# Two mixture-of-experts stages put into a written order, with image pairs on halves of the TensorE array

## The chip, the cores and the metric

The kernel runs on one core of a Trainium2 chip. The metric is the device time of one execution in microseconds (us). The kernel before has a median of 12985.0 us over three runs (12982.07 to 13003.0). One further execution was taken by the profiler; all views of the profile come from it, and its own time is 12885.25 us.

## What is computed

The reference is a network of four layers on an image batch of shape 4 x 128 x 48 x 48: a state-space convolution block (layer 0), a deformable convolution (layer 1), then a linear-attention block with a mixture of experts (layer 2) and a causal attention with a second mixture of experts (layer 3). The change is in the two mixtures alone. Both compute, on tokens t (4 images, L = 2304 tokens, 128 channels), t + experts(norm(t)):

```python
logits = einsum('bsd,ed->bse', x, gate_w) + gate_b        # 64 experts
probs = softmax(logits, axis=1)                           # over the tokens
vals, idx = top_k(probs.transpose(0, 2, 1), 8)            # 8 tokens per expert
pooled = einsum('bked,bke->bed', gathered, topv)
h = gelu(einsum('ebd,edh->ebh', [pooled, 1], weight1))    # hidden size 512
out = einsum('ebh,eho->ebo', [h, 1], weight2)
outputs[b, idx] += out * topv
```

Each expert so weighs its eight tokens of an image into one vector, sends it through its own two matrices, and adds the result back to these tokens. The last mixture writes the network's output, with channels ahead of tokens.

## The kernel before

All arithmetic is in f32. The residual T stays in SBUF as 72 tiles of 128 tokens x 128 channels (18 tiles per image). `program` runs layer 0, layer 1, layer 2, `experts` for "f2_", layer 3 and `experts` for "f3_". The layers 2 and 3 stand in a section `manual_schedule(engines=ORDERED)`, in which TensorE (PE), ACT, DVE and POOL issue in the order of the program; SP, which issues most DMAs, isn't in that set. `_experts` (L1567) stands outside such a section in the kernel before: a scheduler merges its instructions by priority. Its steps are:

- **Gates**, image by image, in blocks of 384 tokens (three tiles; six blocks per image). `moments` (L973) takes bn_stats and bn_aggr of each of 18 tiles on DVE (L980, L981) and the power -0.5 on POOL (L984). ACT normalises each tile to xh (L1605), PE turns three tiles (L1612), DVE copies them to xT (L1614), PE multiplies by the 64 gate columns (L1616) into one half of PSUM's partitions, and ACT adds the bias and writes the logits G (L1617). Images 2q and 2q+1 share G[:, q, :], 64 partitions each.
- **Selection**, per pair q: maximum (L1626), exponential with its sum on ACT (L1629), scaling by 1/sum (L1631), the eight largest (L1634), match_replace and a subtraction that leaves the eight largest and zeros (L1636, L1637), 18 transposes of G with copies to GT on ACT (L1642, L1643), and 18 products per image that pool the tokens (L1648). A product in f32 is two passes on PE, so the profile counts it twice; a transpose is one.
- **Groups**: 64 experts in 16 groups of four. Per group 1 MB each of w1 and w2 is loaded (L1660, L1663, four buffers each). The four experts stand on four strips of 32 columns: w1 product (L1668), bias product with b1 (L1677), Gelu on ACT (L1679), four transposes (L1682), copy hT on DVE (L1684), w2 product (L1688), bias product with b2 (L1697), copy o4 on ACT (L1699), one transpose (L1701) and a copy into oT on DVE (L1702).
- **Output**, per pair, image and block. Each product takes one image's 64 rows of G and o. In "f2_" three products of 64 rows (L1718) are added to T on DVE (L1725). In "f3_" three tiles of T are turned (L1729) and one product (L1737) is accumulated on them in PSUM; the sum is copied on DVE or ACT and goes out by a DMA (L1745).

Of the kernel before, what the change touches and what calls it, by code (L numbers as in the profile page):

```python
# [15 lines left out]
F32 = mybir.dt.float32  # L16
I32 = mybir.dt.int32
AF = mybir.ActivationFunctionType
ALU = mybir.AluOpType
# [4 lines left out]
P = 128  # L24
NB = 4
# [944 lines left out]
            nc.scalar.activation(T[:, b * NT + i, :], out, AF.Relu)  # L970


def moments(env, pool, src):  # L973

    nc = env.nc
    n = src.shape[1]
    st = pool.tile([P, n, nc.vector.BN_STATS_DIM], F32, name="bn_st", tag="bn_st")
    mv = pool.tile([P, n, nc.vector.BN_AGGR_DIM], F32, name="bn_mv", tag="bn_mv")
    for i in range(n):
        nc.vector.bn_stats(out=st[:, i, :], in_=src[:, i, :])  # L980
        nc.vector.bn_aggr(out=mv[:, i, :], in_=st[:, i, :])  # L981
    rstd = pool.tile([P, n], F32, name="rstd", tag="rstd")
    nc.vector.tensor_scalar_add(rstd, mv[:, :, 1], 1e-5)
    nc.gpsimd.tensor_tensor(rstd, rstd, env.half[:, :n], ALU.pow)  # L984
    return mv[:, :, 0], rstd


def normed_T(env, sp, ps, src, mean, rstd, i0, out, scale=1.0, bias=None):

    nc = env.nc  # L990
# [576 lines left out]
def _experts(ctx, env, io, pre, T, final):  # L1567
# [10 lines left out]
    def psum(*shape):  # L1578
        return ps.tile(list(shape), F32, name="psum", tag="ps")
# [12 lines left out]

    xh = cp.tile([P, NB * NT, C], F32, name="xh")
    G = cp.tile([P, npair, L], F32, name="G")
    for b in range(NB):
        Tb = T[:, b * NT : (b + 1) * NT, :]
        mean, rstd = moments(env, sp, Tb)
        shift = sp.tile([P, NT], F32, name="shift")
        nc.vector.scalar_tensor_tensor(shift, mean, -1.0, rstd, op0=ALU.mult, op1=ALU.mult)
        half = slice(b % 2 * NE, (b % 2 + 1) * NE)  # L1600
        for j in range(NBLK):
            pt = psum(P, BLK)
            for g in range(G3):
                i = j * G3 + g
                nc.scalar.activation(  # L1605
                    xh[:, b * NT + i, :],
                    Tb[:, i, :],
                    AF.Identity,
                    bias=shift[:, i : i + 1],
                    scale=rstd[:, i : i + 1],  # L1610
                )
                nc.tensor.transpose(pt[:, bass.ts(g, P)], xh[:, b * NT + i, :], ident)  # L1612
            xT = sp.tile([P, BLK], F32, name="xT")
            nc.vector.tensor_copy(xT, pt)  # L1614
            pg = psum(P, BLK)
            nc.tensor.matmul(pg[half, :], gate_w, xT, start=True, stop=True)  # L1616
            nc.scalar.activation(  # L1617
                G[half, b // 2, bass.ts(j, BLK)], pg[half, :], AF.Identity, bias=gate_b[half, :]
            )

    pooled = cp.tile([P, NE, QC], F32, name="pooled")
    nc.gpsimd.memset(pooled, 0.0)
    for q in range(npair):
        p = G[:, q, :]
        mx = sp.tile([P, 1], F32, name="mx")
        nc.vector.reduce_max(mx, p, axis=AX.X)  # L1626
        nc.vector.tensor_scalar_mul(mx, mx, -1.0)
        total = sp.tile([P, 1], F32, name="total")
        nc.scalar.activation(p, p, AF.Exp, bias=mx, accum_out=total)  # L1629
        nc.vector.reciprocal(total, total)  # L1630
        nc.vector.tensor_scalar_mul(p, p, total)  # L1631

        top = sp.tile([P, TOPK], F32, name="top")
        nc.vector.max(out=top, in_=p)  # L1634
        rest = sp.tile([P, L], F32, name="rest", bufs=1)
        nc.vector.match_replace(out=rest, in_to_replace=top, in_values=p, imm_value=0.0)  # L1636
        nc.vector.tensor_sub(p, p, rest)  # L1637
        GT = sp.tile([P, NT, P], F32, name="GT", bufs=1)
        for j in range(NBLK):
            pt = psum(P, G3, P)  # L1640
            for g in range(G3):
                nc.tensor.transpose(pt[:, g, :], p[:, bass.ts(j * G3 + g, P)], ident)  # L1642
            nc.scalar.copy(GT[:, j * G3 : (j + 1) * G3, :], pt)  # L1643
        for r in range(2):
            b = 2 * q + r
            pp = psum(P, NE)
            for i in range(NT):
                nc.tensor.matmul(  # L1648
                    pp,
                    xh[:, b * NT + i, :],  # L1650
                    GT[:, i, r * NE : (r + 1) * NE],
                    start=i == 0,
                    stop=i == NT - 1,
                )
            nc.vector.tensor_copy(pooled[:, :, b], pp)

    oT = cp.tile([P, NB, NE], F32, name="oT")
    for e0 in range(0, NE, EG):
        w1 = wp.tile([P, EG, HID], F32, name="w1")
        nc.sync.dma_start(w1, w1_io[e0 : e0 + EG, :C, :].rearrange("e d f -> d e f"))  # L1660

        w2 = wp.tile([P, EG, NHC, C], F32, name="w2")
        nc.sync.dma_start(  # L1663
            w2, w2_io[e0 : e0 + EG, :HID, :].rearrange("e (f c) o -> f e c o", c=NHC)
        )
        ph = psum(P, HID)
        for g in range(EG):
            nc.tensor.matmul(  # L1668
                ph[g * QC : (g + 1) * QC, :],
                pooled[:, e0 + g, :],  # L1670
                w1[:, g, :],
                start=True,
                stop=False,
            )
        for g in range(EG):
            own = ident[:NE, e0 + g : e0 + g + 1].to_broadcast([NE, QC])
            nc.tensor.matmul(ph[g * QC : (g + 1) * QC, :], own, b1, start=False, stop=True)  # L1677
        h = sp.tile([P, P, NHC], F32, name="h")
        nc.scalar.activation(h.rearrange("p f c -> p (f c)"), ph, AF.Gelu)  # L1679
        pt = psum(P, NHC, P)  # L1680
        for c in range(NHC):
            nc.tensor.transpose(pt[:, c, :], h[:, :, c], ident)  # L1682
        hT = sp.tile([P, NHC, P], F32, name="hT")
        nc.vector.tensor_copy(hT, pt)  # L1684
        po = psum(P, C)
        for c in range(NHC):
            for g in range(EG):
                nc.tensor.matmul(  # L1688
                    po[g * QC : (g + 1) * QC, :],
                    hT[:, c, g * QC : (g + 1) * QC],  # L1690
                    w2[:, g, c, :],
                    start=c == 0,
                    stop=False,
                )
        for g in range(EG):
            own = ident[:NE, e0 + g : e0 + g + 1].to_broadcast([NE, QC])
            nc.tensor.matmul(po[g * QC : (g + 1) * QC, :], own, b2, start=False, stop=True)  # L1697
        o4 = sp.tile([P, C], F32, name="o4")
        nc.scalar.copy(o4, po)  # L1699
        pt = psum(P, EG, QC)  # L1700
        nc.tensor.transpose(pt.rearrange("p g t -> p (g t)"), o4, ident)  # L1701
        nc.vector.tensor_copy(  # L1702
            oT[:, :, e0 : e0 + EG].rearrange("p b e -> p e b"), pt[:, :, :NB]
        )
    for q in range(npair):
        pt = psum(P, C)
        nc.tensor.transpose(pt, oT[:, 2 * q : 2 * q + 2, :].rearrange("p b e -> p (b e)"), ident)
        o = sp.tile([P, C], F32, name="o")
        nc.scalar.copy(o, pt)
        for r in range(2):  # L1710
            half = slice(r * NE, (r + 1) * NE)
            b = 2 * q + r
            for j in range(NBLK):
                i0 = b * NT + j * G3
                if final is None:
                    pp = psum(P, G3, C)
                    for g in range(G3):
                        nc.tensor.matmul(  # L1718
                            pp[:, g, :],
                            G[half, q, bass.ts(j * G3 + g, P)],  # L1720
                            o[half, :],
                            start=True,
                            stop=True,
                        )
                    nc.vector.tensor_add(T[:, i0 : i0 + G3, :], T[:, i0 : i0 + G3, :], pp)  # L1725
                    continue
                pp = psum(P, BLK)
                for g in range(G3):
                    nc.tensor.matmul(  # L1729
                        pp[:, bass.ts(g, P)],  # L1730
                        T[:, i0 + g, :],
                        ident,
                        is_transpose=True,
                        start=g == 0,
                        stop=False,
                    )
                nc.tensor.matmul(  # L1737
                    pp, o[half, :], G[half, q, bass.ts(j, BLK)], start=False, stop=True
                )
                res = sp.tile([P, BLK], F32, name="res", bufs=4)  # L1740
                if j % 2:
                    nc.scalar.copy(res, pp)
                else:
                    nc.vector.tensor_copy(res, pp)
                nc.sync.dma_start(final[b][:, bass.ts(j, BLK)], res)  # L1745


def layer3(env, io, T):
# [480 lines left out]
```

## Time and profile before

| what | us |
|---|---|
| median of three runs | 12985.0 |
| the profiled execution, its own time | 12885.25 |
| its span, first to last instruction | 12883.3 |
| PE busy, share of the span | 11151.3, 87% |
| DVE busy | 8493.7, 66% |
| ACT busy | 6929.4, 54% |
| POOL busy | 4401.5, 34% |
| first experts stage, first bn_stats to last addition to T | 10733.2 to 11024.6 |
| layer 3 | to about 12563 |
| last experts stage, first bn_stats to the end | 12563.6 to 12883.3 |

The page divides the span into 40 slices of 322 us; the two stages are slices 34 and 40. Busy time on PE is modelled from the size of an instruction, so a busy PE isn't a PE at its peak. "PEclk" or "clock" is the share of TensorE's full clock that was granted in a stretch; it is 0.935 over the span. In a row of a group, "128*64 128x384" is a stationary operand of 128 rows and 64 columns, with an output of 128 partitions x 384 elements. The "chain" is the work that ended last, followed back from the last instruction: start us, length us, engine, tile and line.

### The profile page before, as it was taken

How to read it: one execution, taken by the hardware profiler on the slowest of the kernel's cores; microseconds unless marked ns; L12 is line 12 of the kernel's file. 1: busy time of each engine (PE TensorE's matmuls, PEld its weight loads, DVE VectorE, ACT ScalarE, POOL GpSimd, SP SyncE). 2: the span in 40 equal slices, each digit the busy share in tenths (PEclk: the TensorE clock that was granted, in tenths of full speed). 3: DMA queues.
4: the chain of work that ended last, by engine and by line, in shares of the span. 5: the costliest groups of instructions: out<-in, count | busy, mean ns of one | idle time of the engine just before them, and what ended most of it. 6: DMA issues, size and time to landing. Idle time of an engine off the chain costs nothing. (4 is left out here: it accounts for less than half of the span.)

```text
span 12883.3 us, 192724 instructions
## 1 busy us (share of the span) xinstructions
PE 11151.3 (87%) x71150; PEld 8431.5 (65%) x71150; DVE 8493.7 (66%) x15424; ACT 6929.4 (54%) x13281; POOL 4401.5 (34%) x4727
## 2 busy tenths in 40 slices
PE   6879788878797887689799999999999997899997
PEld 4667666766676666488677787777877774333333
DVE  4998889888988899455555666566665653444442
ACT  3777777777777777311155655555565653123322
POOL 1443333333333344277643333333333331000000
PEclk9999999999999999799899999999999997799995
DMA  2221222122212222266500000000000003000003
GB/s 104 67 71 63 77 79 71 63 77 80 71 63 75 81 67 67 85 189 197 149 1 3 3 4 2 4 3 3 4 2 3 1 1 117 10 6 7 7 8 120
DMA packets 307846, 677.49 MB, mean 53 GB/s; under 512 B 39109, under 2 KB 128985, under 8 KB 304865
## 3 DMA queue, kind: packets, MB, share of 16 engines
q1 hardware_dynamic: 254032, 493.49, 12.2%
q0 software_dynamic: 51840, 169.91, 4.7%
q8 instruction: 571, 9.36, 0.3%
q14 instruction: 363, 2.97, 0.1%
q10 hardware_dynamic: 1040, 1.77, 0.0%
HBM read 602.63 MB, written 71.85 MB: 52 GB/s over the span
## 5 line engine op out<-in xcount | busy, mean ns | idle before, releaser
L565 ACT ACTIVATE hs<-ps,bct 128x256 f32<-128x256 f32 x4608 | 1853.9, 474 | 1182.0 <-PE ps L559 1130.5
L559 PE MATMUL ps<-ident,h 128*128 128x128 f32 x9216 | 1496.1, 294 | 778.8 <-DVE h L545 608.8
L559 PEld LDWEIGHTS ps<-ident,h 128*128 128x128 f32 x9216 | 1083.0, 148 | 1162.5 <-DVE h L545 716.2
L573 PE MATMUL yp<-ident,hs 128*128 128x128 f32 x9216 | 1408.2, 289 | 28.5 <-ACT ys L588 28.5
L505 ACT ACTIVATE dA<-delta,l_Al 128x768 f32<-128x768 f32 x1536 | 1388.3, 936 | 0.3
L512 POOL TENSOR_TENSOR h<-du,rB 128x512 f32<-128x512 f32 x768 | 1077.5, 1403 | 767.5 <-PE ps L559 689.0
L573 PEld LDWEIGHTS yp<-ident,hs 128*128 128x128 f32 x9216 | 1159.9, 151 | 82.7 <-ACT ys L588 57.6
L545 DVE TENSOR_TENSOR_SCAN h<-dA,h 128x256 f32<-128x256 f32 (+1 forms) x1024 | 1083.4, 1058 | 27.2
L545 DVE TENSOR_TENSOR_SCAN h<-dA,carry,h 128x768 f32<-128x768 f32 x512 | 1027.9, 2008 | 10.6 <-ACT dA L505 10.6
L1180 POOL TENSOR_TENSOR T<-T,bias 128x384 f32<-128x384 f32 x384 | 383.8, 999 | 1560.4 <-DVE fn L1108 1520.2
L487 POOL TENSOR_SCALAR_AFFINE_SELECT dB<-bct 128x512 f32<-128x512 f32 x768 | 748.4, 975 | 385.5 <-PE b L519 244.9
L1953 ACT ACTIVATE pT<-scT 128x768 f32<-128x768 f32 (+2 forms) x504 | 377.6, 749 | 894.2 <-PE scT L1945 894.0
L519 PE MATMUL b<-dB,duT 128*128 128x128 f32 x6144 | 830.2, 279 | 0.8 <-ACT duT L445 0.8
L545 DVE TENSOR_TENSOR_SCAN h<-dA,carry,b 128x512 f32<-128x512 f32 x512 | 645.7, 1261 | 267.8 <-PE b L519 250.5
L949 POOL DMA_INDIRECT g<-table,idx x648 | 710.1, 1096 | 263.6 <-issue 146.4
L519 PEld LDWEIGHTS b<-dB,duT 128*128 128x128 f32 x6144 | 770.7, 197 | 2.4 <-POOL h L512 1.2
L962 PE MATMUL pt<-ident,gw 128*128 128x128 f32 x5184 | 661.9, 283 | 103.3 <-DVE gw L956 100.4
L956 DVE TENSOR_TENSOR gw<-g,wq 128x512 f32<-128x512 f32 x648 | 445.9, 694 | 427.9 <-DMA g<-table,idx 377.3
L962 PEld LDWEIGHTS pt<-ident,gw 128*128 128x128 f32 x5184 | 608.0, 193 | 152.1 <-DVE gw L956 119.7
L552 POOL COPY carry<-h 128x2 f32<-128x2 f32 x512 | 97.3, 190 | 1780.4 <-DVE h L545 1715.2
L1901 DVE TENSOR_REDUCE mx<-sc 128x2 f32<-128x1024 f32 (+3 forms) x400 | 428.5, 1071 | 364.8 <-PE sc L1891 359.8
L516 DVE TENSOR_TENSOR h<-du,rB 128x512 f32<-128x512 f32 x768 | 633.3, 825 | 4.2 <-DMA rB<-rows 4.1
(341 smaller groups left out, 23182.1 us busy)
## 6 DMA issues: line engine op xcount, KB each, us to landing
rB<-rows SPq DMA_DIRECT2D x768, 384.0 KB, 3.5
w<-f_w SPq DMA_DIRECT2D x64, 1024.0 KB, 6.4
table<-y SPq DMA_DIRECT2D x9, 2304.0 KB, 17.8
table<-tok SPq DMA_DIRECT2D x16, 1152.0 KB, 10.4
g<-table,idx POOLq DMA_INDIRECT x648, 3.8
xb<-x SPq DMA_DIRECT2D x48, 192.0 KB, 3.1
xn<-xn SPq DMA_DIRECT2D x48, 192.0 KB, 3.5
yd<-y SPq DMA_DIRECT2D x4, 2304.0 KB
```

Of the source, the lines that this page charges most:

```text
L487: nc.gpsimd.affine_select(out=x.dB[n], in_=x.bc[:, m0 : m0 + CT // P, n : n + 1].to_broadcast([P, CT // P, P]), pattern=[[0, CT // P], [1, ...
L505: nc.scalar.activation(dA, x.delta[:, d, :], AF.Exp, scale=A[:, d, x.k, n : n + 1])
L512: nc.gpsimd.tensor_mul(h[:, 1, own], x.du[:, 1, own], x.rB[n][:, own])
L516: nc.vector.tensor_mul(x.h[n][:, :, own], x.du[:, :, own], b)
L519: nc.tensor.matmul(b0[:, bass.ts(m, P)], x.duT[:, m, :], x.dB[n][:, m, :], start=True, stop=True,)
L545: nc.vector.tensor_tensor_scan(h, da, b, initial=first, op0=ALU.mult, op1=ALU.add)
L559: nc.tensor.transpose(tt[:, m, bass.ts(d, P)], x.h[n][:, d, bass.ts(2 * q + m, P)], ident)
L565: nc.scalar.activation(hs, tt[:, m, :], AF.Copy, scale=x.bc[:, 2 * q + m, NS + n : NS + n + 1])
L573: nc.tensor.matmul(yp[:, q, (2 * d + m) * P : (2 * d + m + 1) * P], hs[:, bass.ts(d, P)], ident, is_transpose=True, start=n == 0 and m == ...
L949: nc.gpsimd.indirect_dma_start(out=g, out_offset=None, in_=table, in_offset=bass.IndirectOffsetOnAxis(ap=idx[:, j : j + 1], axis=0),)
L956: nc.vector.tensor_mul(gw, g.rearrange("p (q c) -> p q c", c=C), wq[:, i, t, :].unsqueeze(2).to_broadcast([P, 4, C]),)
L962: nc.tensor.matmul(pt[:, t - t0, :], gw[:, q, :], ident, start=q == 0, stop=q == 3)
```

## The change

`_experts` is written anew and put into a section `manual_schedule(engines=ORDERED)`; `moments` goes. Nothing is changed in the layers. The new order is:

- the statistics (`measure`) of images 0 and 1; then the gates of pair 0 with the statistics of images 2 and 3 between them; then the gates of pair 1 with the selection of pair 0 between them; then the selection of pair 1;
- `gates(q)` works on a block of both images of a pair in each step and is staggered: it normalises block j+1, turns block j and projects block j-1. Of three tiles one is normalised on ACT, one on DVE and one on POOL. The two projections of a pair stand next to each other in the program and fill columns 0 to 63 and 64 to 127, and one activation of 128 partitions adds the bias;
- `select(q)` takes the maximum from the eight largest logits, takes their exponentials beside those of all tokens, compares these, and scales by 1/sum after the subtraction; subtraction and scaling go in thirds, each ahead of the transposes that need it;
- the group loop issues hidden(n), output(n-1), turned(n), keep(n-1);
- in "f3_", T is turned under the group loop: 24 blocks of three transposes with a copy, alternating between DVE and ACT, into tT, which takes the place of xh;
- the outputs of a pair's two images are issued alternately, on rows 0 to 63 and 64 to 127; in "f3_" a DVE addition of tT and PSUM takes the place of accumulation and copy; the result has two buffers per image, shared with xT.

The core of the new code (the bodies of `measure`, `select`, `hidden`, `output` and `keep` hold the operations that the old code had, but for the changes named):

```diff
+    def gates(q):
+        def norm(j):
+            for r in range(2):
...
+                for g in range(G3):
...
+                    if g == 0:
+                        nc.scalar.activation(dst, src, AF.Identity, bias=shift, scale=scale)
+                        continue
+                    (nc.vector if g == 1 else nc.gpsimd).tensor_scalar(
+                        dst, src, m["mv"][:, i, 0:1], scale,
+                        op0=ALU.subtract, op1=ALU.mult,
+                    )
+        def turn(j):
+            for r in range(2):
+                pt = psum(P, BLK)
+                for g in range(G3):
+                    nc.tensor.transpose(pt[:, bass.ts(g, P)], xh[:, i, :], ident)
+                xT = sp.tile([P, BLK], F32, name=f"xT{r}")
+                if r:
+                    nc.scalar.copy(xT, pt)
+                else:
+                    nc.vector.tensor_copy(xT, pt)
+        def project(j):
+            pg = psum(P, BLK)
+            for r, xT in enumerate(t.pop(j)):
+                nc.tensor.matmul(
+                    pg[r * NE : (r + 1) * NE, :], gate_w, xT, start=True, stop=True
+                )
+            nc.scalar.activation(G[:, q, bass.ts(j, BLK)], pg, AF.Identity, bias=gate_b)
...
+        def keep(j):
+            a = bass.ts(j // 2, 2 * BLK)
+            if j % 2 == 0:
+                nc.vector.tensor_sub(p[:, a], p[:, a], t["rest"][:, a])
+                nc.vector.tensor_scalar_mul(p[:, a], p[:, a], t["total"])
+            pt = psum(P, G3, P)
+            for g in range(G3):
+                nc.tensor.transpose(pt[:, g, :], p[:, bass.ts(j * G3 + g, P)], ident)
+            nc.scalar.copy(t["GT"][:, j * G3 : (j + 1) * G3, :], pt)
...
+    with tc.manual_schedule(engines=ORDERED):
+        both(measure(0) + measure(1), [])
+        both(gates(0), measure(2) + measure(3))
+        both(gates(1), select(0))
+        both(select(1), [])
+        if final is not None:
+            tT = cp.tile([P, NB * L], F32, name="tT", tag="xh")
+        for n in range(NE // EG + 1):
+            new = Group(n * EG) if n < NE // EG else None
+            if new:
+                new.hidden()
+            if last:
+                last.output()
+            if new:
+                new.turned()
+            if last:
+                last.keep()
+            while tT is not None and turns * (NE // EG) < NB * NBLK * n:
+                turn_T(tT, turns)
+                turns += 1
+            last = new
+        for q in range(npair):
...
+            for j in range(NBLK):
+                pp = [psum(P, BLK) for r in range(2)]
+                if final is None:
+                    for g in range(G3):
+                        for r, half in enumerate(halves):
+                            nc.tensor.matmul(
+                                pp[r][:, bass.ts(g, P)],
+                                G[half, q, bass.ts(j * G3 + g, P)], o[half, :],
+                                start=True, stop=True,
+                            )
+                    for r in range(2):
+                        nc.vector.tensor_add(dst, dst, pp[r])
+                    continue
+                for r, half in enumerate(halves):
+                    nc.tensor.matmul(
+                        pp[r], o[half, :], G[half, q, bass.ts(j, BLK)], start=True, stop=True
+                    )
+                for r in range(2):
+                    res = sp.tile([P, BLK], F32, name="res", tag=f"xT{r}")
+                    nc.vector.tensor_add(res, tT[:, bass.ts(b * NBLK + j, BLK)], pp[r])
+                    nc.sync.dma_start(final[b][:, bass.ts(j, BLK)], res)
```

`both(a, b)` issues two lists of steps in even alternation.

## The prediction

> **What bounds the kernel now.** I read the page for the whole, then the chain that ended last, to find what carries the two expert stages (first: 10733 to 11025 us; last: 12563 to the end). Nothing else changes: the program's order on every engine is the same before, between and after these stages. So the sum is over 291.4 us and 319.7 us of a span of 12883.3 us. Next came a table of busy time by stage, with the granted clock, in the columns stage, length, PE, PEld, DVE, ACT, POOL (busy us, instructions), clock, DMA share, GB/s.
>
> ```profile
> 10742.00:10818.00 76.00, 55.05 (x116) 18.35 (x117) 29.43 (x135) 41.16 (x93) 9.65 (x3) 0.50 0.21 76
> 10818.00:10857.00 39.00, 24.57 (x189) 22.51 (x191) 22.32 (x19) 14.09 (x21) 0.00 (x0) 0.74 0.00 1
> 10857.00:10900.00 43.00, 29.75 (x386) 12.67 (x386) 5.92 (x13) 5.77 (x13) 0.00 (x0) 1.00 0.89 296
> 10900.00:10992.00 92.00, 73.47 (x590) 27.81 (x590) 7.94 (x19) 8.02 (x19) 0.00 (x0) 0.50 0.41 137
> 10993.00:11024.00 31.00, 30.40 (x145) 29.67 (x145) 12.76 (x23) 0.46 (x2) 0.00 (x0) 0.50 0.00 1
> ...
> 12822.00:12880.00 58.00, 57.77 (x122) 24.72 (x122) 6.69 (x12) 5.85 (x14) 0.00 (x0) 0.50 0.22 78
> ```
>
> These are gates, selection, the group loop (43 + 92) and output; the last stage repeats them, with the longer output of the last row. No engine is full in gates and groups; the outputs are full on PE, at half clock. Inside one group the chain shows why PE idles, at full clock and then at half:
>
> ```profile
> 10889.29 1.00 PE psum L1668 x8
> 10890.29 1.04 PE psum L1677 x8
> 10891.40 0.61 ACT h L1679
> 10892.05 0.77 PE psum L1682 x4
> 10892.84 0.70 DVE hT L1684
> 10893.59 1.08 PE psum L1688 x32
> 10894.67 0.40 PE psum L1697 x8
> ...
> 10907.37 0.60 ACT h L1679
> 10908.02 1.14 PE psum L1682 x4
> 10909.18 0.70 DVE hT L1684
> 10909.93 1.94 PE psum L1688 x32
> ```
>
> A group takes 6.4 us at full clock and 9.85 at half; Gelu, the copy of hT, the copy of o4 and their hops leave PE idle for 1.9 us each time. In the gates each block of 3.02 us is likewise serial: three transposes 0.85, copy of xT 0.57, two passes of the projection 1.54. A product in f32 is two passes. Do halves of the array run side by side on this chip? Attention in layer 3 does both kinds in this trace, at clock 1.00 (scT: two row halves; out: two column halves):
>
> ```profile
> 12540.76 0.80 PE out L1974 x4
> 12541.56 0.84 PE scT L1945 x4
> ```
>
> Four passes of 384 columns in 0.80 to 0.84, where the lone halves of L1616 take 1.54 for two at clock 0.50, so 0.77 for two at full clock: side by side, four cost the time of two.
>
> **The change part by part**, first with the group loop at full clock.
>
> *Start.* Statistics of two images stand on DVE before the first norm. 36 pairs at 0.26 (L980 to L980) are 9.4; DVE waits twice for the pow on POOL (L984, 3.2 plus hops 0.15, with two small DVE operations: 3.8). Sum 17, instead of the 9 to 9.5 until the first xh now. 8 us lost per stage. Images 2 and 3 go under the gates of pair 0.
>
> *Gates of pair 0.* Six steps of two blocks. PE at half clock: 6 transposes 1.3, two side-by-side passes 1.3, two changes of shape at 0.14 (0.35 from the last transpose's start to the product, less 0.21): 2.9, so 17.5 for six. DVE has more: 12 norms at 0.28 = 3.3, 6 copies of xT at 0.555 = 3.3, 36 pairs = 9.4, twice 3.8 of waiting for pow with norms and copies queued behind it = 7.6: 23.6, with the pipeline's ends 25. POOL: 12 norms at 0.794 (the same operation is in the profile, kn at L1108 on POOL) and two pows = 16, hidden. DVE carries it: **25**.
>
> *Gates of pair 1 with selection of pair 0.* The selection stands in DVE's and ACT's order: max 2.55, exp 0.2 + 2.4 (with ACT's norms and copies behind it), match_replace 2.55, first subtraction and scaling of a third (0.85 + 0.5), with hops 9.4 before PE can pass the first transposes of G, which stand ahead of the next turn in PE's order. Then PE has 18 transposes for G and 30 for gates, 12 side-by-side passes and one pooling: 27 at half clock, 14 at full; ACT 6 x (0.97 + 0.49 + 0.58 + 0.49) = 15. Between them I take 9.4 + 21.6 = **31**, bounds 25 (ACT alone) and 37 (PE at half clock). reduce_max (2.55 each) goes; the scaling of p is only moved.
>
> *Selection of pair 1.* Last gate to pooled: G 0.6, max 2.6, exps 2.7, rest 2.6, first third 1.4, 18 transposes 4.2 (DVE feeds six in 1.35), pooling 8.0 at full clock (72 passes at 0.11): 22, with the copy **23**; 30 with pooling at half. Start, gates and selection now take 124 us; 17 + 25 + 31 + 23 = 96.
>
> *Groups.* Between hidden(n) and turned(n) stands output(n-1), 1.48 long: Gelu's 0.6 plus hops fits. The copy of o4 (0.27) lies under turned(n) (0.76), that of hT (0.69) under hidden(n+1) (2.03). If this cover fails, the 1.9 comes back. PE alone then: 1.00 + 1.04 + 0.76 + 1.08 + 0.40 + 0.25 = 4.5 at full clock, 8.0 at half (1.86 + 1.91 + 1.14 + 1.94 + 0.63 + 0.48). What is late next is the weights: 12 of 16 groups of 2.1 MB are loaded in the loop. The trace moved up to 329 GB/s beside this loop and 387 in the opening burst: 5.4 to 6.4 us a group. With four groups of buffers ahead, the last group's weights come at 64 to 75 us, where PE wants them at 68. 72 for PE, a few for the weights, 3 to drain: **80** instead of 135. The last stage adds 4.5 transposes a group (72 for T, 0.11 to 0.12 each, and a change of shape): 0.5; with copies of tT on ACT and DVE far from full (each about 1.3 a group): **88**.
>
> *The clock* decides more than any of these. The Trainium skill (TensorE: Matmul & The Clock Gate, Why this matters for your kernels) says to keep TensorE busy for 4 us to get full clock. The first stage's output row has PE busy 30.4 of 31 us, the last one's 57.8 of 58, both at 0.50. So here busy time is not enough; both use half the rows. I therefore count how full the array is (an estimate): a full pass of 128 columns takes 0.107 us at full clock (0.213 at 0.50). A group holds hidden 0.86, biases on half the rows 0.43 + 0.05, output 0.86, five transposes 0.53: 2.75. That is 0.43 of 6.4 us: the loop holds full clock for 43 us and loses it; 0.28 of 9.85: it never comes back. 18 transposes in 3.97 us (0.49) bring full clock before both loops. The edge is near 0.4. After: 2.75/4.5 = 0.6, and 0.5 even at the weights' slowest likely pace, so full clock stays once it is there. Entered at half clock, it is 0.34 (0.40 with T's transposes): it may not rise. By the rule, 80 and 88 are certain; by the rows they need the transposes of G dense over most of one stretch of the gate (3.4 us by that page's Part 1). Now they follow thirds from DVE, so dense for about 4.2 us with small gaps. Two in three I give it per loop, more with T's transposes.
>
> *Outputs.* First stage: 6 side-by-side products per step; PE 1.28 at half clock, 0.66 at full; DVE's two additions 2 x 0.555 = 1.11. Twelve steps at 1.2 and a lead of 1.8: **16** instead of 32. Last stage: one side-by-side product, 1.3 or 0.65; DVE 1.1; two buffers per image, each held for addition 0.56, issue 0.33, landing 1.9 and hops: 1.5 a step. 12 x 1.5 + 1.8 + the last landing 2.2 = **22** instead of 60.8. The transposes of T, at 0.85 per block, leave this stage.
>
> *Sum.* First: 96 + 80 + 16 = 192 instead of 291, gain 99. Last: 96 + 88 + 22 = 206 instead of 320, gain 114. Together 213; I keep 8 for hand-overs not listed: 205. The profiled execution has 12885.25 us (span 12883.3), the median of the runs 12985.0, 0.8% more, which nothing in the trace explains; I carry the gain over in us: 12985 - 205 = **12780**.
>
> **Rivals.**
> *One loop enters at half clock:* loop 131 instead of 80 (or 150 instead of 88), pooling +7: 58 or 69 lost, gain some 140: 12845. For it: DVE now feeds the transposes. Against: both loops now enter at 1.00. *Both:* gain 78, 12907.
> *Weights become the bound:* at 6.4 us a group from the start of the loop, 12 x 6.4 + 8 = 85 to 90 each, little lost by itself, 12790 to 12800; but the idle time lowers the filling to 0.43, as now, and the clock may go late in the loop. This lies in the range.
> *The halves exclude each other (slower).* If two halves took turns with load and product end to end, a pass of the first output would cost 0.33 + 0.42 (means of L1718's load and product) instead of 0.209 apart: 144 x 0.75 = 108 instead of 31. Gates: 48 passes x 1.06 = 51, transposes 18, selection's waits 22: 91, beside the start's 17. The array, never full, keeps the loops at half: first 17 + 91 + 30 + 131 + 108 = 377 (+86), last 17 + 91 + 30 + 150 + 56 = 344 (+24): 13095. It becomes slower than now once a pass of a half costs about 0.4 more than side by side. The two rows of attention speak against it.
>
> **How the numbers follow.** Both loops at full clock, the weights' rival with it: 0.60, 12780 (12755 to 12810). One at half: 0.24. Both at half: 0.10. Halves exclude each other: 0.03. Waits in the gates that eat nearly all: 0.03, of which 0.02 within 0.2%. The bounds of pair 1's gates (25 to 37, twice) move the likeliest case by -12 and +12. The range 12750 to 12880 takes the first two cases and leaves 0.16 to 0.18. Faster by over 0.2% (some 26 us, about what this measurement can tell from no change): 0.95; within: 0.02; slower: 0.03.
>
> **What would show it.** A group every 4.5 to 5.4 us at clock 1.00 with hT's wait gone; gate products starting in pairs; x4 groups of the first output within one pass's time; the first gate transposes 17 us after the stage's first statistics, DVE waiting for POOL four times a stage; outputs of 16 and 22 us. Wrong, if the clock row reads 0.50 in a group loop, if PE waits for DMA w in it, or if the gates of pair 1 take over 40.

## The result, and the profile after

In the runs that were timed together, the changed kernel takes 12768.15 us (median of four, 12761.87 to 12774.82) beside 12985.78 us for the kernel before (four runs): a ratio of 0.983, with a 95% interval of 0.9814 to 0.9846, or 217.6 us less. Its profiled execution has a span of 12767.5 us and an own time of 12769.64 us.

The two profiled spans are only 116 us apart, so they must not simply be subtracted. Layer 1, whose instructions and order are the same in both kernels, took 910.7 us in the profile of before (first to last instruction of L962) and 1007.1 us in that of after. This difference of 96 us has nothing to do with the change; the last section comes back to it. The change is read from its own two stages:

| us | first stage, before | after | last stage, before | after |
|---|---|---|---|---|
| first statistics to the first product of the groups | 123.8 | 105.3 | 123.0 | 105.6 |
| groups, to the first product of the output | 136.3 | 77.6 | 136.7 | 78.6 |
| output | 31.4 | 13.3 | 60.1 | 19.6 |
| whole stage | 291.4 | 196.2 | 319.7 | 203.8 |

The stages gain 95.2 and 115.9 us, 211 together. The same by the table of busy time in stretches of the first stage of after, with the columns of the table of before:

```profile
10838.00:10875.00 37.00, 15.63 (x61) 7.65 (x61) 25.87 (x130) 11.09 (x25) 18.59 (x15) 0.64 0.34 125
10875.00:10905.00 30.00, 18.65 (x118) 12.79 (x118) 16.97 (x31) 16.08 (x33) 10.87 (x13) 0.76 0.00 1
10931.00:11008.00 77.00, 67.30 (x980) 31.23 (x979) 12.71 (x32) 13.68 (x32) 0.00 (x0) 1.00 0.91 329
11009.00:11023.00 14.00, 10.35 (x146) 9.71 (x145) 11.33 (x24) 0.53 (x2) 2.70 (x3) 0.87 0.11 24
```

The rows are about the gates of pair 0, those of pair 1, the groups and the output. In the third, all 16 groups run at clock 1.00, where before 92 of 135 us had 0.50. It has 980 instructions on PE in 77 us; before it took two rows, 43 and 92 us, for 976. DMA moves 329 GB/s there, the pace that the prediction had feared as the next bound. The chain that ended last shows one group of after:

```profile
10939.51 1.00 PE psum L1740 x8
10940.51 0.99 PE psum L1748 x8
10941.50 1.01 PE psum L1765 x32
10942.51 0.35 PE psum L1773 x8
10942.86 0.68 PE psum L1757 x4
10943.54 0.11 PE psum L1781
```

Hidden, output of the group before, turned, keep: six PE entries with no gap, 4.14 us. The entries of ACT h and DVE hT that stood in before's chain are gone, because each of them now runs under products of another group.

### The profile page after: what moved, and what is told of

It is laid out like the page before. It is cut to its first block, busy times and chain, and to the rows that moved or that the text cites. A ratio compares the mean times of both kernels' runs of the same rounds, so it can differ in the third digit from the quotient of the medians.

```text
span 12767.5 us, 192717 instructions
## 1 busy us (share of the span) xinstructions
PE 10986.9 (86%) x71150; PEld 8409.7 (66%) x71150; DVE 8483.4 (66%) x15484; ACT 6895.6 (54%) x13189; POOL 4394.0 (34%) x4775
## 4 chain that ended last, share of the span: by engine, by line
PE 43%; DVE 7%; ACT 3%; issue 1%; DMA 1%; POOL 1%; another core or an unknown queue 0%; SPq 0%; ACTq 0%; DVEq 0%; POOLq 0%
PE psum L1425 4%; PE pt L962 4%; PE psum L1417 4%; PE pc L1311 3%; PE psum L1361 3%; PE scT L2061 3%; PE sc L2007 3%; PE out L2090 3%; PE psum L1331 2%; PE psum L1171 2%; PE psum L1172 2%; PE psum L1105 2%; PE psum L1249 1%; PE psum L1350 1%; DVE mx L1334 1%
## 5 line engine op out<-in xcount | busy, mean ns | idle before, releaser
L962 PE MATMUL pt<-ident,gw 128*128 128x128 f32 x5184 | 677.1, 292 | 167.7 <-DVE gw L956 139.0
L949 POOL DMA_INDIRECT g<-table,idx x648 | 656.9, 1014 | 412.4 <-DVE gw L956 179.4
L962 PEld LDWEIGHTS pt<-ident,gw 128*128 128x128 f32 x5184 | 642.2, 205 | 197.3 <-DVE gw L956 133.5
L956 DVE TENSOR_TENSOR gw<-g,wq 128x512 f32<-128x512 f32 x648 | 425.7, 692 | 494.1 <-PE pt L962 420.6
```

The source lines that it names most:

```text
L949: nc.gpsimd.indirect_dma_start(out=g, out_offset=None, in_=table, in_offset=bass.IndirectOffsetOnAxis(ap=idx[:, j : j + 1], axis=0),)
L962: nc.tensor.matmul(pt[:, t - t0, :], gw[:, q, :], ident, start=q == 0, stop=q == 3)
```

## The experiments

Each kernel is the changed one with one edit, but for the two unedited kernels run again. They ran in three sets. The kernel before, run beside each set, had a median of 12896.4 us in the first and third and 12992.5 us in the second; absolute times compare within a set only. The changed kernel itself ran in the second set; for the others "the changed kernel beside it" is an estimate, 12896.4 - 211 = 12685.

### 1. The kernel before and the kernel after, again

> The kernel before once more, with a profile. The two profiled executions differ by 116 us in span, the medians by 217. Theory A: the difference lies in layer 1, whose instructions the change leaves alone: there the profiled execution of before took 911 us from the first to the last transpose of L962 and the one of after 1007. If layer 1 has two paces whatever the kernel, this execution is expected with either 911 (span near 12883) or 1007 (span near 12980), and with expert stages of 291 and 320 us in both cases. Theory B: the change itself slows layer 1: then layer 1 is at 911 here, and in every execution of this kernel.

> The changed kernel once more, beside the kernel before on the same chip. If layer 1 has a pace of its own in each session, the difference of the medians stays at the sum of the two stages' gains, 95 + 116 = 211 us, with layer 1 near 910 us here: near 12685 beside 12896.

The kernel before: span 12879.4 us, layer 1 in 912.0, stages 291 and 320 as in its first profile. Both group loops lost the clock again 42.8 us after their first product; the first one had it back for 3.4 us and lost it for good at 53.1. The kernel after: 12781.3 us, ratio 0.9836 (0.9818 to 0.9854), stages 197.3 and 203.3, so the gain of 211 repeats. But its layer 1 took 1030.7 us, where I had expected 910. So the slow layer 1 came again with the changed kernel and the fast one with the kernel before, and it takes the other sets to tell what it goes with; that is taken up at the end.

### 2. The stagger taken away

> The changed kernel with each group's steps in a row (hidden, turned, output, keep), all else as in the change. Theory A (the stagger hides Gelu and the copies, and the array filled by it holds the clock): in the first stage 6.4 us a group at full clock and 9.85 after the clock is lost, so a loop near 135 us instead of 76.6; in the last stage T's transposes fill the array some more (0.47 of 6.9 us): 110 us if the clock holds, 155 if not, instead of 78. Together 12768 + 90 to 135 = 12860 to 12905. Rival 1 (the weights' transfers bound the loop anyway): both loops stay within 5 us, 12770. Rival 2 (the clock follows idle gaps, and these are below 1 us each): full clock all through, 103 and 110 us, 12825.

```diff
             if new:
                 new.hidden()
-            if last:
-                last.output()
-            if new:
                 new.turned()
-            if last:
-                last.keep()
+                new.output()
+                new.keep()
```

12794.63 us, ratio 0.9924 (0.9907 to 0.994): about 110 us above the changed kernel. The loops take 136.6 and 143.5 us. The first, by stretches:

```profile
10839.00:10882.00 43.00, 29.65 (x393) 12.78 (x389) 5.95 (x13) 5.77 (x13) 0.00 (x0) 1.00 0.89 295
10882.00:10975.00 93.00, 73.89 (x591) 27.82 (x583) 8.08 (x19) 8.07 (x20) 0.00 (x0) 0.50 0.41 136
```

These are the two rows of before almost digit for digit, with all of the other edits in place: the 43 us at full clock, then 93 at half. So the order within the loop alone carries that loop's gain. The last loop, which also turns T, lost its clock after 46.5 us, got it back, and lost it four times more, 20.5 us or one and a half times that apart; its 143.5 us lie between the two cases expected (110 and 155).

### 3. The same, with the idle time filled

> The unstaggered kernel with twelve more transposes of 128 x 128 per group, whose results nobody reads: six behind hidden and six behind turned, where TensorE waits for Gelu and for hT. Theory A (the clock follows how full the array is, edge near 0.4): 12 x 0.107 = 1.3 us more of a full array in 6.4 us make 0.63, the clock holds at 1.00, and the loops take 103 to 108 and 110 to 115 us: faster than unstaggered by some 30 us in the first stage, with more work. Rival (the clock falls for another cause, such as the time since the stage began or TensorE being busy too long): the same loss of clock at some 43 us, and the loops are no shorter than unstaggered, or longer by up to 16 x 1.3.

```diff
                 new.hidden()
+                filler(6)
                 new.turned()
+                filler(6)
                 new.output()
                 new.keep()
```

`filler(6)` is six transposes of full 128 x 128 tiles into PSUM that nobody reads: 192 extra PE instructions per stage, no result. 12729.9 us, ratio 0.9876 (0.986 to 0.9893), 65 us *faster* than the same order without that work. The first loop:

```profile
10835.00:10878.00 43.00, 39.56 (x474) 21.36 (x470) 5.96 (x13) 5.78 (x13) 0.00 (x0) 1.00 0.90 297
10878.00:10939.00 61.00, 55.04 (x698) 30.02 (x698) 7.99 (x19) 8.04 (x19) 0.00 (x0) 1.00 0.62 206
```

The first 43 us move as fast as without filler (297 against 295 GB/s), with the clock now staying at 1.00 to the end: 105.1 and 112.7 us. This splits the gain of the loop. As an estimate from these times: of the 59 us that the stagger takes from the first loop, the clock is some 34 (136.6 less 16 groups of 6.4 us at full clock, 102) and the cover of Gelu and copies some 25 (102 less 77.6).

### 4. Outputs image by image

> The changed kernel with the outputs issued one image after the other, so that two halves of rows never stand next to each other. Theory A (side by side halves the passes' time and fills the array): the first output has half an array at work, falls to clock 0.50 and takes 144 x 0.209 = 30 us instead of 14; the last one 48 x 0.64 = 31 instead of 20.5. Together +26: 12794. Rival (DVE's additions carry the outputs, 24 x 0.555 = 13.3 us, and TensorE at full clock would keep pace even with half an array): +0 to +6.

```diff
-                    for g in range(G3):
-                        for r, half in enumerate(halves):
+            for r in range(2):
+                half = slice(r * NE, (r + 1) * NE)
...
+                for j in range(NBLK):
...
-                                pp[r][:, bass.ts(g, P)],
+                                pp[:, bass.ts(g, P)],
```

The two halves of the rows now meet only where image 1 follows image 0, as in the kernel before. I had expected outputs of about 30 us; that was wrong. 12691.7 us, ratio 0.9847 (0.983 to 0.9863); outputs of 17.2 and 20.5 us, 4 and 1 more than side by side. The first one:

```profile
10918.00:10935.00 17.00, 16.05 (x145) 15.54 (x145) 12.96 (x24) 0.27 (x1) 0.40 (x2) 1.00 0.00 1
```

It has the instruction counts of before's output (x145), in half the PE time (16.05 against 30.40 us) at clock 1.00. It enters at full clock from the staggered loop and keeps it for its 17 us. Whether it would keep it for longer isn't shown. So I tried the same output behind a loop that ends at half clock:

### 5. Outputs image by image behind the loop without stagger

> Unstaggered groups, so that the first output is entered at clock 0.50, and the outputs issued one image after the other. With side by side halves the same entry gave 14.1 us in the first output at a mean clock of 0.81; with the halves apart, but entered at 1.00, it took 17.2 us. Theory A (at half clock half an array fills 0.25, which never brings the clock up; side by side fills 0.5, which does): 30 to 31 us at clock 0.50 in the first output, and about 31 to 33 in the last if it is entered at 0.50 as well. Rival (the clock rises with TensorE being busy without gaps): it rises within a few us, and the first output takes about 19.

The edits of 2 and 4 together: 12818.4 us, one run. With one run its time is not compared; what counts is its trace. Its first output, then that of experiment 2, which is side by side behind the same half clock:

```profile
10970.00:11001.00 31.00, 30.09 (x145) 29.28 (x144) 13.16 (x24) 0.27 (x1) 0.35 (x1) 0.50 0.00 1
```

```profile
10976.00:10989.00 13.00, 10.63 (x143) 10.13 (x139) 11.20 (x24) 0.27 (x1) 1.78 (x3) 0.82 0.06 14
```

Apart, PE is busy 30.09 of 31 us and stays at 0.50 throughout. Side by side, the same products bring the clock up within the stretch. So two halves at once count as a fuller array, and one half, busy for 31 us, did not lift the clock.

The last output of this run is a second case. It too was entered at 0.50, but took 24 us and not the 31 to 33 expected, because the clock rose after 8.8 us:

```profile
12792.00:12801.10 9.10, 8.83 (x18) 5.19 (x19) 3.46 (x7) 0.22 (x2) 0.00 (x0) 0.50 0.30 108
12801.10:12808.00 6.90, 6.54 (x25) 3.86 (x24) 4.96 (x11) 0.27 (x1) 0.00 (x0) 1.00 0.72 257
```

This isn't one half lifting the clock. From 12797.6 us on, the first four passes of image 1 start between the last four of image 0 (0.64 us a pass), so for some 2.5 us both halves are at work; 1 us later the clock rises. In the first output the same meeting of the images lasts 0.85 us (passes of 0.21), and the clock did not rise. So the program's order alone does not keep the halves apart where the images meet.

In the changed kernel, though, this side is needed little: its loop already delivers the full clock.

### 6. Gate projections apart

> The changed kernel with the two projections of a pair parted by the six transposes of the next step, so that they can't run side by side; all else as in the change. Theory A (the written order and the stagger carry the gates; DVE and ACT are later than TensorE there): the projections cost 0.64 more a step at full clock and up to 1.3 at half, but only some of it is on the path: +2 to +8 a stage, +4 to +16 in all against the change on the same chip. Rival (side by side is what makes the gates shorter): 12 steps x 1.5 = +18 a stage and more, if the clock stays at half: +36 or more.

```diff
+            if j > 0:
+                project(j - 1)
             if 0 <= j < NBLK:
                 turn(j)
             if j > 0:
-                project(j - 1)
+                project_other(j - 1)
```

Here `project` is cut down to the image on columns 0 to 63; `project_other` does that on 64 to 127, and the bias.

12688.79 us, ratio 0.9847 (0.9812 to 0.9882); stages 202.5 and 207.0, that is 6.3 and 3.2 longer. The last G of pair 1 comes 85.1 and 83.2 us after the first statistics, not 78.1 and 78.4. A small gain of the adjacent projections, as expected where DVE carries most of this phase. How the rest of what gates and selection gain (18.5 and 17.4 us a stage) splits between the norms on three engines, the stagger and the maximum that is gone was not tried.

### 7. T turned in the last output again

> The changed kernel with T turned in the last output again, accumulated under the product as before, and copied on DVE and ACT; nothing of T in the last group loop. Theory A (in the loop the transposes lie under the wait for weights, so that leaving them out gains under 2 us; at full clock the output takes 6 x 0.11 + 0.66 + changes of shape 0.3 = 1.6 us a step on TensorE, as long as its buffers take): loop 77, output 20 to 23, in all 0 to +4. Rival (turning T under the loop is what brings the last output from 60 to 20): output 35 or more.

T's transposes leave the last loop and go into the output, accumulated under the product as in the kernel before. 12673.29 us, ratio 0.983 (0.9794 to 0.9866); the last loop 77.4 us, its output 23.6, the stage 206.7: 2.9 more than in the changed kernel. The time itself, some 12 below the estimate for the changed kernel, tells no more than that such an estimate across sets is good to about 10 us; the reading is taken from the stage. Turning T under the groups is worth some 3 us.

### 8. Statistics with producer and consumer apart

> The changed kernel with the statistics of three tiles issued as three bn_stats and then three bn_aggr. In the change each bn_aggr stands right behind its own bn_stats, and pairs follow each other every 0.40 us on DVE, not every 0.26 as before. Theory (an instruction that needs the result of the one just ahead of it on DVE waits for its end): pairs at about 0.29, so the first gate products come 4 us earlier and the gates of pair 0 end 3 us sooner still: -7 a stage, -14 in all. Rival (the interval comes from contention with the weights' transfers in that stretch): no change.

In the timeline of DVE in the changed kernel, the pairs of statistics start 0.40 us apart, not the 0.26 of before:

```profile
10826.95 0.26 DVE L1598 BATCH_NORM_STATS2 st<-T 128x6 f32<-128x128 f32 x1
10827.25 0.18 DVE L1599 BATCH_NORM_AGGREGATE mv<-st 128x2 f32<-128x6 f32 x1
10827.35 0.26 DVE L1598 BATCH_NORM_STATS2 st<-T 128x6 f32<-128x128 f32 x1
```

The bn_aggr starts 0.30 us after its bn_stats, behind whose end it stands in the same queue, and needs its result. In the kernel before, the scheduler had put another tile's bn_stats between:

```profile
10733.67 0.26 DVE L980 BATCH_NORM_STATS2 bn_st<-T 128x6 f32<-128x128 f32 x1
10733.84 0.17 DVE L981 BATCH_NORM_AGGREGATE bn_mv<-bn_st 128x2 f32<-128x6 f32 x1
10733.92 0.26 DVE L980 BATCH_NORM_STATS2 bn_st<-T 128x6 f32<-128x128 f32 x1
```

```diff
             for i in range(i0, i0 + G3):
                 nc.vector.bn_stats(...)
+            for i in range(i0, i0 + G3):
                 nc.vector.bn_aggr(...)
```

12757.26 us, 24 below the changed kernel beside it; ratio to before 0.9829 (0.981 to 0.9848). The stages are 10.4 and 8.9 us shorter (7 expected), which rules out the weights' transfers as the cause. The timeline has three tiles every 0.78 us:

```profile
10836.12 0.68 DVE L1598 BATCH_NORM_STATS2 st<-T 128x6 f32<-128x128 f32 x3
10836.72 0.30 DVE L1600 BATCH_NORM_AGGREGATE mv<-st 128x2 f32<-128x6 f32 x3
10836.94 0.65 DVE L1598 BATCH_NORM_STATS2 st<-T 128x6 f32<-128x128 f32 x3
```

### 9. The maximum of pair 1 ahead of the pooled copy

> The changed kernel with the copies of the pooled tokens issued one step later, so that the maximum of pair 1 stands ahead of the copy that waits for the last pooling of pair 0. Theory (DVE's order holds the maximum back by 3.7 us, from the last gates at 10905.2 to 10908.9): -3.7 a stage, -7 in all. Rival (the selection of pair 1 waits for TensorE's pooling anyway): within 1 us.

In the changed kernel DVE stands idle ahead of the copy of the pooled tokens (in brackets: the idle time and its releaser), and the maximum of pair 1 stands behind it in the program:

```profile
10908.77 0.27 DVE L1712 COPY pooled<-psum 128x64 f32<-128x64 f32 x1 [4.68 <-PE psum L1705]
10908.91 2.55 DVE L1674 MAX8 top<-G 128x8 f32<-128x2304 f32 x1
```

The edit makes the copy a step of its own, one later, with the maximum ahead of it. The groups start 4.8 and 3.5 us sooner (expected 3.7). The time, 12773.09 us, ratio 0.9837 (0.9818 to 0.9856), is 8 us below the 12781.3 beside it; by the stages it is 5.7 and 0.3 (7 expected in all). In the last stage the loop gave 3 us back:

```profile
12654.00:12722.00 68.00, 65.19 (x891) 32.44 (x890) 15.95 (x38) 16.61 (x37) 0.00 (x0) 1.00 0.99 354
12722.00:12735.00 13.00, 12.54 (x164) 7.15 (x160) 2.85 (x7) 2.47 (x6) 0.00 (x0) 0.76 0.26 96
```

Sixty-seven us into the loop the clock fell, although PE was busy 65 of the 68 us before. The idle time lies right ahead of the fall, where PE waits for the weights of its last group:

```profile
12720.12 1.07 PE L1743 MATMUL psum<-w,pooled 128*32 128x512 f32 x8 [1.74 <-DMA w<-f_w]
```

The changed kernel idles there ahead of three groups, for 0.5, 0.7 and 0.9 us, and keeps the clock. This is the end that the prediction gave to its rival of the weights: idle time lowers the filling, and the clock goes late in the loop.

### 10. Both together, and the wait for POOL covered

> Both of these together, and each shift (which waits on DVE for the power on POOL) issued two steps later, so that the statistics of the next image run under that wait, with the last shift behind the maximum. Each of four waits of 3.4 us a stage is then covered but for that of image 1. Theory (these are waits in the written order, not work): -7 - 3.7 - 3.4 - 3.4 - 2.5 = -20 a stage, -40 in all. Rival (TensorE or ACT is next at once in the gates): -15 to -25 in all.

The edits of 8 and 9; besides, the `shift` of an image, which waits for the power on POOL, goes two steps later in DVE's order, so that the next image's statistics run in between:

```profile
10840.91 0.18 DVE L1607 SCALAR_TENSOR_TENSOR shift<-mv,rstd 128x18 f32<-128x18 f32 x1 [1.90 <-POOL rstd L1604]
10847.77 0.18 DVE L1607 SCALAR_TENSOR_TENSOR shift<-mv,rstd 128x18 f32<-128x18 f32 x1 [3.33 <-POOL rstd L1604]
```

Of image 0's wait 1.90 us is left, where the changed kernel has 3.47; that of image 1 has nothing to hide under; of those of images 2 and 3 (3.4 each) 0 and 0.5 are left. 12745.43 us, ratio 0.9815 (0.9798 to 0.9833); stages 180.7 and 187.3, together 33 us below the changed kernel's 197.3 and 203.3 in the same set (40 expected). The median lies 36 below. This is the fastest version, 1.85% below the kernel before.

## Why the prediction was right, and where it was off

The kernel became faster by 217.6 us by the medians and by 211 by its stages; the prediction had 205, the time 12780, and the measured 12768 lies in its range. Step by step:

**The groups were right, their size a little too long.** The sum gave 4.5 us of PE per group and 80 and 88 us per loop. A group takes 4.14 us, because the entries of the chain follow each other with no loss at a change of shape, and the loops 77.6 and 78.6. Near its end the first loop is bound by the weights, as the rival said; a wait for DMA w in a loop was among the prediction's signs of being wrong, and it came without that:

```profile
L1740 PE MATMUL psum<-w,pooled 128*32 128x512 f32 x128 | 17.1, 603 | 8.1 <-DMA w<-f_w 7.7 <-DVE pooled L1712 0.4
```

PE waits 7.7 us in all for w (16 x 4.14 = 66, and the wait, and the drain: 77). The filling did not fall far enough to lose the clock within the loop. T's transposes cost the last loop 1 us and not 8, since they lie where PE would wait for weights: it idles 2.4 us ahead of w1 products there, and 7.6 with the transposes taken out (experiment 7).

**The clock was right, and experiments 2, 3 and 5 show why; the edge was not.** The Trainium skill (TensorE: Matmul & The Clock Gate, Why this matters for your kernels) asks to keep TensorE busy. Here the staggered order makes it busier and fuller at once, so the changed kernel alone can't tell the two apart. Experiment 5 does: 30.09 of 31 us busy with half the rows, at 0.50. By the count of the prediction, experiment 2 fills 0.43 of the array at full clock and loses it; with filler it is (2.75 + 12 x 0.107)/6.57 = 0.61 and keeps it; the changed kernel has 2.75/4.14 = 0.66. But the last loop of experiment 2, with T's transposes, has 0.47 and lost it as well. So an edge of 0.4, counted over whole groups, is too low.

The traces on record allow a finer count. In all thirteen, the changes of the clock lie whole numbers of 3.41 us apart. I mean by filling, as an estimate, each pass's share of the 128 x 128 array over its time, with a pass at half clock counted half, summed over one such stretch as a share of it. The two stages of the thirteen traces have 1705 stretches. All 104 that a fall follows are filled 0.355 or less, and an edge of 0.365 puts all but 12 of the 1705 right, where the best edge for PE's busy time leaves 369 wrong. It tells why the clock falls late: in the first loop of before the stretches vary from 0.38 to 0.52, as a group of 6.4 us lies differently over each, and 39.5 us in one has 0.30. The fall in experiment 9 comes behind a stretch of 0.34. This count was made after the experiments, and none was run to test it.

Three readings of the prediction were off here without changing what it forecast. The last output of before uses all the rows for T's transposes (by its count 0.27 of the array, at half clock); the bias with b2 fills 0.11, not 0.05; and a loop with T's transposes at half clock would have 0.36, not 0.40, because the transposes also take time.

**The outputs were right in size (16 and 22 predicted, 13.3 and 19.6 measured), by another split.** I had the gain come from the halves side by side. Experiment 4 takes that away and gives back only 4 and 1 us: the first output gains mostly because it inherits the full clock. At half clock the halves would have been worth much more: 31.5 us apart and 14.1 side by side (experiments 5 and 2). The last output is also free of T's transposes and of the long accumulations; its buffers hold it, as predicted:

```profile
12759.12 2.03 DMA out<-res
12761.28 0.57 DVE res L1860
12761.86 1.89 DMA out<-res
```

Each addition waits for the landing of the transfer that held its buffer.

**Gates and selection are the mis-sized term: 105.3 and 105.6 us, where the sum had 96.** In the first stage:

| term | predicted | measured |
|---|---|---|
| start, to the shift of image 1 | 17 | 21.9 |
| gates of pair 0 | 25 | 23.0 |
| gates of pair 1, selection of pair 0 | 31 | 33.7 |
| selection of pair 1 | 23 | 26.6 |

The start used 0.26 us a pair, from before's rows. That figure belonged to an order in which a result is not needed by the next instruction: 36 x (0.40 - 0.26) = 5.0 us, all of the 4.9 that are missing, and experiment 8 gets them back. The step "the selection of pair 1: 22 with the copy 23" forgot a queue: the maximum stands behind the pooled copy, which waits for PE. That holds it back by 3.7 us, all of the 3.6 that are missing, and experiment 9 gets them back. (The first gate transpose comes after 11.7 us, not 17: image 0 need not wait for image 1.) In the gates of pair 1 a norm on DVE takes 0.34, not 0.28, and a third of the subtraction 0.95, not 0.85; that is about 1 of the 2.7 us missing there, and the rest is open.

So the sum was met in part by luck: over both stages, gates and selection are 18.9 us longer than forecast, and loops and outputs 16.9 us shorter. The 8 us kept for hand-overs were not needed.

**The rivals.** The loops were never entered at half clock here, so its price (131 or 150 us) was not measured in the changed kernel; experiment 2, which falls to half by itself, had 136.6. The halves do not exclude each other: in the timeline, the two gate products take, at full clock,

```profile
10890.60 0.87 PE L1652 MATMUL psum<-xT,gate_w 128*64 128x384 f32 x4
```

that is four passes in 0.87 us, where excluding halves need two times 0.77.

**The unexplained 0.8%** of the prediction (12985 beside an own time of 12885) is most likely layer 1; no trace of before was taken in a set in which it needs 12985 us. It took 905 to 912 us in the first profile of before (own time 12885) and in all seven of the first and third sets, in which the kernel before had 12896, six of them of edited versions of the changed kernel. It took 1007 to 1031 us in the five profiles of sets in which the kernel before had 12986 to 12993. So layer 1's pace goes with the set of runs and not with the program.

## What to carry to other kernels

Before moving work on TensorE for cover, count what the array is filled with at each stage, in stretches as short as those in which the clock moves, and look at the granted clock there: an order that closes the gaps can pay twice, for the cover and for the clock, and here the second was the larger part of the loop. A duration taken from a row holds for the neighbours that it had there: when an order is written by hand, put a producer and its consumer on one engine apart, and look at what stands behind each waiting instruction. Compare stage by stage, since an untouched stage can differ by some 100 us between two profiles, half of what the change moves here.

## What the runs showed of the hardware that was not expected

- The clock changes only at steps of 3.41 us and, by the estimate above, goes by how full the array was in the step before, with an edge near 0.365. A loop that fills 0.43 on average so keeps the full clock for some 43 us, until one step falls on a thin part: 42.8 to 42.9 us after the first product in all four loops of the kernel before that were traced, and 43.0 in experiment 2.
- Useless work made a kernel 65 us faster (experiment 3).
- Layer 1 has two paces. The granted clock between 5430 and 6330 us is 0.99 in the trace of before and 0.94 in that of after. VectorE's products (L956) show different waits in the two, by releaser, in before's profile and then in after's:

```profile
  DMA g<-table,idx: 377.3, 492
```

```profile
  PE pt L962: 420.6, 252
```

  The second line can't be taken as a cause. The five traces with the slow pace give no landing time for the gathers of g (the other eight have 3.8 us), so a wait for one of them may stand there under another name. What sets the pace was not tried, and no experiment here separates the chip that a set ran on from its state at the time.
